# Mask loads moved from the POOL queue to the SP queue in a two-layer masked attention kernel

## The chip, the cores and the metric

The kernel runs on one NeuronCore of one Trainium2 chip. The metric is device time in microseconds (us) of one execution. A profile is one execution recorded instruction by instruction; its span runs from the first to the last instruction. The engines are PE (matrix multiply), PEld (its weight loads, which overlap it), DVE (vector), ACT (scalar, activations), POOL (GpSimd) and SP, which here issues transfers and nothing else. Transfers are issued from the instruction streams of SP, POOL and ACT, in the order in which each stream holds them.

## The reference

Sixteen graphs of 1024 nodes with 256 features, each with a 1024x1024 matrix of 0 and 1, go through two layers of attention. In both the input is normalised and passed through a ReLU, and a score counts only where the matrix is not 0. Layer 0 has 4 heads of 64, layer 1 has 8 heads of 32. All numbers are 32-bit floats; the adjacency is 32-bit integers.

```python
def layer(x, adj, H, Wq, Wk, Wv, Wo, bo):
    h = jnp.maximum(_layernorm(x), 0.0)
    q, k, v = heads(h @ Wq), heads(h @ Wk), heads(h @ Wv)     # layer 1 adds biases
    s = jnp.where(adj > 0, einsum('bhnd,bhmd->bhnm', q, k) / sqrt(256 / H), -inf)
    o = einsum('bhnm,bhmd->bhnd', softmax(s), v)
    return x + concat(o) @ Wo + bo
```

## The kernel before

**Steps.** The attention of one graph is cut into groups: two halves of 512 queries (`qh` 0 and 1) times two groups of heads (`g` 0 and 1). A group runs over its keys in steps of four 128x512 score blocks, 4 steps a group in layer 0 and 8 in layer 1, so a graph has 16 steps of layer 0 and 32 of layer 1. The order of all 768 steps is: layer 0 of graph 0, then, for each graph b, layer 0 of graph b+1 followed by layer 1 of graph b. A period is therefore 48 steps: 16 of layer 0, then 32 of layer 1. In the code `a` is the step at which a period's layer 0 begins, `c = a + 16` the one at which its layer 1 begins; this text counts steps as a+n and c+n. In layer 0 two steps are handled at once and called a pair here.

**A step.** PE computes scores into PSUM (line 454), DVE combines them with the mask (line 477) into a tile p, ACT takes the exponential in place (line 483), and two steps later PE multiplies p with the values (line 495). Scores share three PSUM pairs with every other product, so PE's next scores wait until DVE has read older ones. The row sums of p, which the softmax divides by, come from adding p tiles: on DVE and POOL in layer 0 (lines 504 to 510), on POOL in layer 1 (line 608), where further tiles are added by an accumulating DMA (`accumulate`, line 591) before PE sums over keys (`count`, line 347). `spread`, `invert`, `fetch` and `normalize` (lines 363 to 406) then carry the sums through DRAM: SP transfers sums, vd and inv, and POOL multiplies the head outputs `cat` by inv (line 406). `end_half` (line 431) multiplies by Wo, adds to x and, in layer 1, stores the result (line 444).

**The masks.** A graph's mask comes in eight parts. `Mask.load` (line 143) fetches one part, `put` (line 156) turns it on ACT into an 8-bit form for layer 0, `flip` (line 169) transposes it in blocks on DVE, `second` (line 172) rewrites it on ACT for layer 1. The load is a DMA of the POOL queue that converts 32-bit integers to bf16 as it moves them, into one of two buffers of the pool `adjp`. The first graph's eight parts go to two `p` buffers that are still unused.

**Order.** Each step holds a list of further work, filled by `later(step, function, ...)`; `Stream.run` works it off behind the step's exponentials, large products last. Each engine then runs its instructions strictly in the order in which they were written. The step numbers at lines 766 to 819 are set by hand: when a mask part is loaded, put and flipped, when x is loaded (`open_x`, line 132), when its statistics (`stats`, line 186, DVE) and norms (line 207, ACT) are taken. In before, the parts of the mask of graph b+2 are loaded at a+4, a+8, a+12, c+1, c+12, c+16, c+20 and c+24, each put five steps later and flipped one after that. The second half of x of graph b+2 is loaded at a+14, and the first half of its statistics stands at c (at c+3 in the first period).

**The first accumulating DMA.** In `count_steps` (line 594) a group's first accumulating DMA is issued at its step j=3, with the POOL additions of that step, except in the group with `qh` and `g` both 0: there it is put at the head of the list two steps later.

## Time and profile before

| what | value |
|---|---|
| time, median of 3 runs | 3191.39 us (3191.0 to 3192.33) |
| the profiled execution's own time | 3184.43 us |
| its span | 3182.7 us, 45121 instructions |
| PE busy | 3119.6 us, 98% |
| POOL / DVE / ACT busy | 80% / 79% / 70% |
| mask loads on POOL (line 149) | 128, 207.6 us busy |
| mask puts on ACT (line 164) | 128, 145.2 us busy |
| mean granted PE clock | 0.997 |

A row of the groups gives a line's busy time and the mean duration of one instruction, then the idle time of its engine just before it and what ended it. A row of the timeline gives start and duration in us, engine, line, operation, output and inputs, the number of merged instructions, and in brackets the idle time before it with its releaser. A fp32 product counts as two instructions, and ends of products are modelled, so PE is best read from start to start: the time from one row's start to the next row's start is what the first one took of PE. A window's row gives the window, its length, and the busy time and instructions of PE, PEld, DVE, ACT and POOL in it, then the granted PE clock, the share of the DMA engines and GB/s.

### The profile page before, as it was taken

Reading aid. Unit: us, or ns where it says so; the run is one execution under the profiler, and the core shown is the slowest. Engines: PE = TensorE matmul, PEld = TensorE weight load, DVE = VectorE, ACT = ScalarE, POOL = GpSimd, SP = SyncE. Lnnn points to the kernel's source line nnn. Section 1 sums busy time; section 2 is a strip of 40 time slices with the busy share of each in tenths; the row PEclk is TensorE's granted clock in tenths of the full one; section 3 lists DMA queues with packets and bytes.
Section 4 is the critical chain, followed back from the end, with each engine's and each line's share of the span. In section 5 each row is a group of like instructions: output and inputs, shape, how many; then the busy total and the mean of one; then the engine's idle time right before and its main releaser. Section 6 shows DMA issues by size and latency. Waiting matters only on the chain.

```text
span 3182.7 us, 45121 instructions
## 1 busy us (share of the span) xinstructions
PE 3119.6 (98%) x16662; PEld 1221.8 (38%) x16662; DVE 2521.7 (79%) x2882; ACT 2236.4 (70%) x2440; POOL 2540.5 (80%) x1358
## 2 busy tenths in 40 slices
PE   8989999999999999999999999999999999999998
PEld 3433333434334343333433334333343433434332
DVE  6678788887878878788887878878888787887776
ACT  5657767686676766767677686776768667676765
POOL 5568788797887978878788797878879788796776
PEclk9999999999999999999999999999999999999999
DMA  7216556364563745636355463555636446372421
GB/s 94 34 31 123 105 103 115 76 130 91 104 117 80 132 85 104 126 83 126 85 110 113 89 122 82 113 104 104 115 76 130 91 102 118 83 132 68 87 61 32
DMA packets 449684, 308.46 MB, mean 97 GB/s; under 512 B 248752, under 2 KB 408752, under 8 KB 432432
## 3 DMA queue, kind: packets, MB, share of 16 engines
q0 software_dynamic: 283344, 173.82, 33.8%
q1 hardware_dynamic: 166112, 131.68, 15.1%
q8 instruction: 133, 2.18, 0.3%
q14 instruction: 95, 0.78, 0.1%
HBM read 149.95 MB, written 47.96 MB: 62 GB/s over the span
## 4 chain that ended last, share of the span: by engine, by line
PE 79%; DMA 8%; DVE 7%; issue 2%; SPq 1%; POOL 1%; ACT 1%; DVEq 0%; POOLq 0%; ACTq 0%
PE ps L454 27%; PE po L495 23%; PE pq L270 11%; PE py L436 7%; PE pv L306 6%; PE pz L347 4%; DMA p<-p 4%; DVE p L477 3%; DMA out_dram<-x 3%; DMA x<-in_x_dram 1%; POOL p L608 1%; DVE p L507 1%; DVE st L195 1%; DVE p L504 1%; SPq L444 1%
## 5 line engine op out<-in xcount | busy, mean ns | idle before, releaser
L483 ACT ACTIVATE p<-p 128x1024 f32<-128x1024 f32 x1536 | 1613.0, 1056 | 722.0 <-DVE p L477 662.1
L477 DVE SCALAR_TENSOR_TENSOR p<-mask,ps 128x1024 f32<-128x1024 fp8e5 x1536 | 1786.2, 1214 | 373.8 <-PE ps L454 360.0
L608 POOL TENSOR_TENSOR p<-p,p 128x1024 f32<-128x1024 f32 x510 | 1217.8, 2449 | 135.9 <-PE po L495 115.8
L454 PE MATMUL ps<-qT,kT 32*128 32x512 f32 (+1 forms) x6144 | 1125.3, 628 | 19.7 <-DVE p L477 15.9
L495 PE MATMUL po<-p,v 128*32 128x512 f32 (+1 forms) x6144 | 981.0, 600 | 3.1 <-ACT cat L358 2.8
L454 PEld LDWEIGHTS ps<-qT,kT 32*128 32x128 f32 (+1 forms) x6144 | 380.8, 184 | 694.9 <-issue 288.8
L495 PEld LDWEIGHTS po<-p,v 128*32 128x32 f32 (+1 forms) x6144 | 233.6, 118 | 684.6 <-issue 468.2
L508 POOL TENSOR_TENSOR p<-p 128x1024 f32<-128x1024 f32 x128 | 302.5, 2363 | 89.0 <-DVE p L507 83.6
L507 POOL TENSOR_TENSOR p<-p,p 128x1024 f32<-128x1024 f32 x64 | 150.7, 2355 | 200.1 <-DVE p L504 120.3
L406 POOL TENSOR_TENSOR cat<-cat,inv 128x512 f32<-128x512 f32 x127 | 193.0, 1566 | 91.9 <-DMA inv<-vd 89.8
L270 PE MATMUL pq<-hT,wk 128*128 128x512 f32 x512 | 238.4, 609 | 2.7 <-DMA hT<-turned 1.6
L306 PE MATMUL pv<-wv,hT 128*128 128x256 f32 x1024 | 237.8, 385 | 0.1
L270 PE MATMUL pq<-hT,wq 128*128 128x512 f32 x512 | 236.6, 605 | 0.1
L436 PE MATMUL py<-wo,cat 128*128 128x256 f32 x1008 | 234.0, 385 | 1.2 <-DVE p L477 1.2
L306 PEld LDWEIGHTS pv<-wv,hT 128*128 128x128 f32 x1024 | 189.4, 190 | 72.1 <-DVE p L477 25.0
L436 PEld LDWEIGHTS py<-wo,cat 128*128 128x128 f32 x1008 | 186.6, 190 | 73.3 <-issue 35.1
L149 POOL DMA_DIRECT2D adj<-in_adj_dram x128 | 207.6, 1622 | 4.6 <-issue 4.0
L504 DVE TENSOR_TENSOR p<-p 128x1024 f32<-128x1024 f32 x128 | 171.0, 1336 | 0.0
L347 PE MATMUL pz<-p,ones 128*32 128x512 f32 x1248 | 163.4, 596 | 7.6 <-DMA p<-p 6.8
L592 POOL DMA_DIRECT2D p<-p x133 | 121.8, 916 | 53.1 <-POOL p L608 19.5
L441 DVE TENSOR_TENSOR x<-py,x 128x1024 f32<-128x1024 f32 x63 | 76.9, 1221 | 101.7 <-PE py L436 100.7
L223 POOL TENSOR_TENSOR x<-x,bo 128x1024 f32<-128x1024 f32 x64 | 156.9, 2512 | 0.0
(51 smaller groups left out, 1750.9 us busy)
## 6 DMA issues: line engine op xcount, KB each, us to landing
p<-p POOLq DMA_DIRECT2D x133, 1024.0 KB, 8.1
adj<-in_adj_dram POOLq DMA_DIRECT2D x128, 256.0 KB, 9.7
turned<-hn SPq DMA_DIRECT2D x58, 512.0 KB, 3.5
hT<-turned SPq DMA_DIRECT2D x232, 128.0 KB, 5.3
x<-in_x_dram SPq DMA_DIRECT2D x128, 128.0 KB, 2.8
inv<-vd SPq DMA_DIRECT2D x128, 128.0 KB, 2.9
inv<-vd SPq DMA_DIRECT2D x252, 64.0 KB, 4.8
out_dram<-x SPq DMA_DIRECT2D x124, 128.0 KB, 2.8
```

Source lines behind the costliest of these rows:

```text
L149: nc.gpsimd.dma_start(at, rows[u // 4, u % 4])
L270: nc.tensor.matmul(pq[:, m, :], wt[self.layer][:, c, ts(m, P)], self.hT[half][:, c, :], start=(c == 0), stop=(c == 1),)
L306: nc.tensor.matmul(pv[:, i, :], self.hT[half][:, c, ts(i, P)], w.v[self.layer][:, c, :], start=(c == 0), stop=(c == 1),)
L347: nc.tensor.matmul(self.s[ts(r, 32), :], w.ones.to_broadcast([P, 32]), of, start=start, stop=stop)
L436: nc.tensor.matmul(py[:, i, :], self.half.cat[:, c, ts(i, P)], w.o[self.layer][:, c, :], start=(c == 0), stop=(c == 1),)
L454: nc.tensor.matmul(st.ps[i // 2][:, i % 2, :], gr.inp.kT[r * D : (r + 1) * D, gr.g, ts(kt, P)], gr.inp.qT[gr.qh][r * D : (r + 1) * D, gr.g ...
L477: nc.vector.scalar_tensor_tensor(out=half, in0=gr.mask.m[gr.qh][:, kt // 4, :, kt % 4].unsqueeze(1).to_broadcast([P, 2, 512]), scalar=-EDG ...
L483: nc.scalar.activation(half, half, AF.Exp, scale=gr.scale)
L495: nc.tensor.matmul(gr.o[r * D : (r + 1) * D, :], gr.inp.v[:, kt, h * D : (h + 1) * D], st.halves[i // 2][:, i % 2, :], start=(kt == 0), st ...
L504: nc.vector.tensor_add(a, a, b)
L508: nc.gpsimd.tensor_add(a, a, b)
L608: nc.gpsimd.tensor_add(half, half, of)
```

## The change

The mask load becomes a plain copy of 32-bit integers issued by SP, into a buffer of 4 KB a partition; with the same memory there is one such buffer where there were two of bf16. `put` reads the integers. The first graph's parts go to four `p` buffers; four of the eight are issued by ACT, four by SP. Loads, puts and flips have new steps: the loads of graph b+2 stand at a+6, a+8, a+10, a+12, a+14, c+29 (of the same period), and a+1, a+3 of the next, each put at the step of the next load, in front of it. All but the one at c+29 stand in a layer 0. `second` is spread more widely. The second half of x is loaded at c, behind the layer 0's `inv` in SP's order, and the first half of its statistics moves from c to c+2. The first accumulating DMA of layer 1 is issued at j=3 in every group. The sums of the last graph, which borrow the mask buffer, follow the new buffer count.

```diff
-    adjp = ctx.enter_context(tc.tile_pool(name="adjp", bufs=2))
+    adjp = ctx.enter_context(tc.tile_pool(name="adjp", bufs=1))
...
-        def load(self, u, at=None):
+        def load(self, u, at=None, by=nc.sync):
 
             if at is None:
-                at = adjp.tile([P, 4, 256], BF16, tag="adj", name=f"adj_{self.b}_{u}")
+                at = adjp.tile([P, 4, 256], I32, tag="adj", name=f"adj_{self.b}_{u}")
             self.src[u] = at
             rows = adj[self.b].rearrange("(t h r g) (k c) -> h t k r g c", h=QH, r=32, g=4, k=4)
-            nc.gpsimd.dma_start(at, rows[u // 4, u % 4])
+            by.dma_start(at, rows[u // 4, u % 4])
...
                 elif j == 3:
-                    if gr.qh or gr.g:
-                        self.accumulate(one, gr.one)
-                    else:
-                        self.due.setdefault(i + 2, []).insert(0, (self.accumulate, (one, gr.one)))
+                    self.accumulate(one, gr.one)
...
-    stage = [pp.tile([P, 4, 4, 256], BF16, tag="p0", bufs=7, name=f"adj_0{i}") for i in range(2)]
+    stage = [pp.tile([P, 2, 4, 256], I32, tag="p0", bufs=7, name=f"adj_0{i}") for i in range(4)]
 
     def load(u):
-        masks[0].load(u, stage[u // 4][:, u % 4])
+        masks[0].load(u, stage[u // 2][:, u % 2], nc.scalar if u < 4 else nc.sync)
...
     for t in range(NT):
         i = 5 + 2 * t
-        later(i - 3, masks[1].load, t)
+        later(i - 2, masks[1].load, t)
         later(i, masks[1].put, t)
-        later(i + 1, masks[1].flip, t)
+        later(i + 2, masks[1].flip, t)
...
-        for i, u in zip((0, 1, 2, 3, 4, 6, 8, 10), range(NT)):
+        for i, u in zip((0, 2, 4, 6, 7, 9, 11, 13), range(NT)):
             later(a + i, masks[b].second, u)
         if b + 2 < B:
             other, mask = inputs[0][b + 2], masks[b + 2]
             later(a + 6, open_x, b + 2, 0)
-            later(a + 14, open_x, b + 2, 1)
+            later(c, open_x, b + 2, 1)
...
-                norms(other, 1, c, c + 4, c + 5, c + 6, bias=c + 36)
+                norms(other, 1, c + 2, c + 4, c + 5, c + 6, bias=c + 36)
                 block_inputs(other, 1, c + 7, c + 8, c + 12, c + 22, c + 26, c + 30)
-            for i, t in zip((9, 13, 17, 22, 33, 37, 41, 45), range(NT)):
-                later(a + i - 5, mask.load, t)
-                later(a + i, mask.put, t)
-                later(a + i + 1, mask.flip, t)
+            at = 6, 8, 10, 12, 14, 45, 49, 51, 53
+            for t in range(NT):
+                later(a + at[t], mask.load, t)
+                later(a + at[t + 1], mask.put, t)
+                later(a + at[t + 1] + (1 if t == 4 else 2), mask.flip, t)
```

More of the change, by code (lines that the diff above doesn't have):

```diff
@@ L368, in spread @@
             if k == 0:
-                pool, tag, bufs = small, f"sums{self.layer}", 1
+                pool, tag = small, f"sums{self.layer}"
                 if self.layer and inp.b == B - 1:
-                    pool, tag, bufs = adjp, "adj", 2
+                    pool, tag = adjp, "adj"
                 inp.sums = pool.tile(
-                    [P, (4 if self.layer else 2) * self.n_f], F32, tag=tag, bufs=bufs,
+                    [P, (4 if self.layer else 2) * self.n_f], F32, tag=tag, bufs=1,
                     name=f"sums_{inp.n}",
```

## The prediction

> **What bounds the kernel now.** I read the page first (which engine is full), then the windows of one period (does the bound change by stage), then PE's timeline from start to start (where PE loses time although it counts as busy), then DVE, POOL and SP around those places. The page:

> ```profile
> PE 3119.6 (98%) x16662; PEld 1221.8 (38%) x16662; DVE 2521.7 (79%) x2882; ACT 2236.4 (70%) x2440; POOL 2540.5 (80%) x1358
> ...
> L149 POOL DMA_DIRECT2D adj<-in_adj_dram x128 | 207.6, 1622 | 4.6 <-issue 4.0
> ```

> PE is the bound. The mask loads are 208 us of POOL, but POOL is idle for a fifth of the span, so that time is not itself on the path. The windows of one period (layer 0 is the first two):

> ```profile
> 915.60:954.40 38.80, 38.80 (x172) 15.31 (x168) 27.81 (x27) 26.04 (x28) 31.09 (x16) 1.00 0.50 98
> 954.40:992.00 37.60, 37.60 (x176) 16.18 (x172) 31.15 (x40) 26.04 (x29) 27.12 (x14) 1.00 0.37 76
> 992.00:1014.00 22.00, 21.23 (x106) 8.10 (x104) 15.96 (x18) 12.53 (x15) 14.93 (x7) 1.00 0.33 103
> 1014.00:1045.00 31.00, 30.52 (x177) 11.69 (x174) 26.21 (x29) 21.46 (x24) 27.10 (x17) 1.00 0.55 109
> 1045.00:1111.00 66.00, 66.00 (x422) 24.40 (x421) 56.92 (x70) 53.22 (x59) 60.03 (x34) 1.00 0.66 118
> ```

> Layer 0 has no idle PE at all; what there is lies in the first 50 us of layer 1. PE's rows there:

> ```profile
> 1001.30 2.26 PE L454 MATMUL ps<-qT,kT 32*128 32x512 f32 x8
> 1003.56 3.72 PE L306 MATMUL pv<-wv,hT 128*128 128x256 f32 x16
> 1008.04 2.26 PE L454 MATMUL ps<-qT,kT 32*128 32x512 f32 x8 [0.76 <-DVE p L477]
> 1010.23 1.92 PE L495 MATMUL po<-p,v 128*32 128x512 f32 x16
> ...
> 1020.73 1.85 PE L454 MATMUL ps<-qT,kT 32*128 32x512 f32 x8
> 1022.58 3.70 PE L270 MATMUL pq<-hT,wq 128*128 128x512 f32 x8
> ...
> 1040.27 1.06 PE L495 MATMUL po<-p,v 128*32 128x512 f32 x8
> 1041.79 1.07 PE L347 MATMUL pz<-p,ones 128*32 128x512 f32 x8 [0.46 <-DMA p<-p]
> ```

> Eight score instructions take 1.07 us from start to start where nothing holds them (1012.09 to 1013.16 us); pv takes 3.65 (961.99 to 965.64). So the rows lose 2.26 − 1.07 = 1.19, 4.48 − 3.65 = 0.83 and 2.19 − 1.07 = 1.12 us at c+2 and c+3, 0.78 us at c+6 (1020.73), and 0.46 us in the wait of the row sums at c+11. The same subtraction over eleven periods gives, per period, 2.2 us at c+2 and c+3, 0.8 at c+6, and 1.5 in four small stalls of 0.37 late in layer 1. Nearly all else runs at PE's pace. DVE and SP say why:

> ```profile
> 999.94 0.43 DVE L195 BATCH_NORM_STATS2 st<-x 128x6 f32<-128x256 f32 x1 [3.31 <-DMA x<-in_x_dram]
> 1004.75 2.11 DVE L507 TENSOR_TENSOR p<-p,p 128x1024 f32<-128x1024 f32 x1
> 1016.88 2.18 DVE L199 TENSOR_TENSOR ve<-mv,numbers 128x4 f32<-128x4 f32 x1
> ...
> 994.47 1.75 SPq L135 DMA_DIRECT2D x<-in_x_dram  x4
> 996.27 0.43 SPq L389 DMA_DIRECT2D vd<-vn  x1
> 999.98 2.40 SPq L398 DMA_DIRECT2D inv<-vd  x4
> ...
> 1003.73 4.26 POOL L406 TENSOR_TENSOR cat<-cat,inv 128x512 f32<-128x512 f32 x2 [6.60 <-DMA inv<-vd]
> ```

> DVE stands still for 3.31 us because x's second half has not landed, and the mask step for c+1 (1001.18 us) is queued behind those statistics. The x load stood in SP's queue until an earlier store had landed (the waits give SP at line 135 100.5 us for out_dram), and vd and inv stood behind it; so POOL waits 6.60 us and its two multiplications then meet DVE's additions.

> **The change part by part** (times per period of about 194 us; fourteen periods load masks, thirteen have the statistics at c.)

> *x's second half and its statistics.* The statistics leave c, so DVE's wait there goes. The next candidate for lateness is PE itself: the scores of c+1 end at about 997.7, so line 477 can start there instead of at 1001.18, 3 us earlier. The x load now follows inv: vd no longer waits behind x, so inv is issued about 3 us earlier (from 999.98), x follows at about 999.5 and lands 2.8 us later (its median), near 1002.5; its first reader stands behind c+2's mask steps, which end not before 1004. The gain is between 0 and 13 × 2.2 = 28.6 us. What can take it back is the meeting of DVE's two additions with POOL's two multiplications, which come earlier too: L507 takes 2.11 us here and 1.22 elsewhere, 0.9 us lost, on a DVE that is now 3 us ahead. I take 1.8 of the 2.2: 23 us.

> *First accumulating DMA.* Its issue moves from c+7 (1033.12 us) to behind the POOL additions that begin at 1020.40 and end at 1025.10, 8 us earlier. It landed 8.1 us after issue (median), just too late; now it lands with 8 us to spare. The page's waits give PE 6.8 us in 13 such waits. The 0.9 us that its issue costs POOL only moves, ahead of additions that wait for PE until 1028.49. Between 0 and 6.8; I take 6.5.

> *The stall at c+6.* DVE is late there because L199, 4 columns wide, took 2.18 us while POOL ran an addition from 1014.35 to 1019.03; L201, as wide, took 0.15. POOL loses its 1.60 us mask load at 1012.73 and starts that addition earlier, and DVE arrives earlier: whether they meet again is open. Between 13 × 0.8 = 10 us gained and, if a block as long arises at a second place, 10 lost. I take half of the gain, 5. [...]

> *Mask loads.* 120 parts leave POOL: 120 × 1.62 = 195 us that PE never waited for; DVE waited for POOL's line 608 only 6.7 us in all. I take 1 us. On SP each load costs an issue of about 0.45 us (the four x issues take 1.75). ACT's puts keep their 1.13 us (no row reads integers; the same instruction takes 1.13 from 8-bit and 1.06 for fp32 exponentials; lower bound nothing changed, upper a few tenths, covered below). Per period five puts and five flips move from layer 1 into layer 0: 5 × 1.14 us of ACT and 5 × 0.43 of DVE. There ACT is busy 26 of 38 us and DVE 28 and 31, and pair by pair a gap takes them: at a+10 ACT idles 1.67 us ahead of the exponentials at 975.29, for a 1.13 us `second`. Cost 0; if the cover goes, up to 5.7 us of ACT per period.

> *Waits that are added.* With one buffer, a load waits for ACT's put of the part before it. Behind the load at a+8 in SP's queue stands inv of the last group (issued at 962.69, with its put now ending at about 962.8): it goes out about 1 us later and POOL's line 406 (969.66) and then the py product (981.07) have 11 us. Behind the load at a+14 stands vd of layer 0 (996.27 before); its put ends near 993. The tightest landing is the load of a+6: it goes out behind x at about 957.2, and its put stands at about 961.65, 4.4 us later; ACT then has 1.5 us idle before line 310. A 512 KB transfer of the SP queue (turned) lands in 3.5 us (2.6 to 5.8), 128 KB of x in 2.8, 256 KB of mask on POOL's queue in 9.7. I take 4, the SP rows being nearest: cost 0. From 5.9 us on it costs PE.

> *The start.* Four issues on ACT, about 0.45 each, lie in its idle 7.30 us before the first norm and 1.42 before the first copy; four SP issues delay x of graph 1, needed only at 48 us. PE runs without a gap from 27 to 38 us with either. Layer 0's stalls up to 330 us (some 12 us above a later period) shift by −5 to +3; I take −1.

> Sum: 23 + 6.5 + 5 + 1 + 1 = 36.5, less 1.5 for ACT and SP delays that I can't place: 35 us. The profiled execution took 3184.4 us, 7.0 below the median of the runs; taken off the median, 3191.4 − 35 = 3156. About 0.2% (6.4 us) is what a measurement here can tell from no change.

> **Rivals.**
> 1. The blocks come back: DVE and POOL meet at c+2 and at c+4 as before, and only the accumulating DMA and half of the x wait show. For it: L199's row. Against it: 3 us of DVE lead. 6.5 + 6.5 = 13: 3178.
> 2. All of it goes, with c+6 entirely and the start's 5 and two of the four 0.37 us stalls, since five puts and flips leave layer 1: 28.6 + 6.8 + 10 + 5 + 14 × 0.74 = 61: 3130. Against it: the same 0.37 stalls recur in the last graph, which loads no masks.
> 3. Slower: the 512 KB loads land late. At the 9.7 us of the old queue, the put at a+8 waits 5.3 us, of which ACT's idle covers 1.5 to 2.8; the put at a+10 follows its load by 9 us and loses about 3.5, the next about 1: some 7.5 us × 14 = 105, less 35: 3261. It decides from a landing of about 5.9 + 2.5 = 8.4 us.

> **How the numbers follow.** Forecast (3143 to 3169) 0.50; rival 1 0.18; rival 2 0.17; rival 3 0.08; changes that nearly cancel 0.04, and small losses 0.03. Rival 1's small side and the cancelling case give 0.07 for the same; rival 3 and the losses 0.11 for slower; faster is 0.82. The range from 3126 to 3186 takes in both nearer rivals and leaves out the late landing.

> **What would show it.** Right: no DVE wait for x at c; inv issued before x and POOL's 6.60 us wait shorter by about 3; the scores at c+2 and c+3 at 1.1 to 1.5 us; no wait of line 347 for p; mask loads landing in 3 to 5 us. Wrong: line 164 waiting for adj, PE idle in layer 0, or L504, L507 or L199 at 2 us in new places.

## The result, and the profile after

The changed kernel takes 3460.78 us (median of 4 runs, 3456.3 to 3469.73) against 3191.19 us before (3190.6 to 3192.33): ratio 1.0848, 95% interval 1.0825 to 1.0870. It is 270 us slower where 35 us faster were predicted. Its profiled execution took 3462.27 us, with a span of 3460.5 us and a mean granted PE clock of 0.966 (0.997 before).

The page of the changed kernel, with the rows that answer to those of before:

```profile
PE 3207.1 (93%) x16662; PEld 1244.7 (36%) x16662; DVE 2526.3 (73%) x2882; ACT 2236.4 (65%) x2440; POOL 2310.9 (67%) x1230
...
L164 ACT ACTIVATE mask<-adj,numbers 128x1024 fp8e5<-128x1024 int32 x128 | 146.6, 1148 | 348.9 <-DMA adj<-in_adj_dram 348.9
```

POOL is relieved as announced (2540.5 to 2310.9 us busy), and `put` costs the same from integers (1148 ns against the 1.13 us assumed). But ACT now waits 348.9 us for mask parts, and PE is idle for 7% of the span (2% before), now in layer 0 too, where the windows of before show none. The windows of one period (window and length; then busy PE, PEld, DVE, ACT, POOL; granted clock, DMA share, GB/s; layer 0 is the first three):

```profile
1002.00:1040.80 38.80, 33.70 (x133) 12.79 (x130) 23.65 (x21) 20.71 (x22) 29.56 (x15) 0.91 0.52 118
1040.80:1078.40 37.60, 31.88 (x135) 13.65 (x135) 24.62 (x30) 22.96 (x24) 13.22 (x7) 0.91 0.35 94
1078.40:1094.50 16.10, 16.10 (x76) 6.67 (x72) 13.09 (x18) 12.03 (x14) 9.61 (x6) 1.00 0.25 74
1094.50:1130.00 35.50, 33.24 (x157) 14.07 (x156) 24.76 (x30) 18.34 (x21) 20.62 (x12) 0.90 0.29 85
1130.00:1217.00 87.00, 86.66 (x545) 31.18 (x543) 72.28 (x83) 65.42 (x74) 72.32 (x40) 1.00 0.52 114
```

Three of the five windows have idle PE and a clock of 0.90 or 0.91. The late part of layer 1 (the last row) is as full as it was. The timeline of ACT and of PE in the second window:

```profile
1052.22 4.51 ACT L483 ACTIVATE p<-p 128x1024 f32<-128x1024 f32 x4 [0.56 <-DVE p L477]
1064.75 1.15 ACT L164 ACTIVATE mask<-adj,numbers 128x1024 fp8e5<-128x1024 int32 x1 [8.01 <-DMA adj<-in_adj_dram]
...
1067.32 1.00 ACT L310 COPY v<-pv 128x1024 f32<-128x1024 f32 x1
...
1075.10 1.15 ACT L164 ACTIVATE mask<-adj,numbers 128x1024 fp8e5<-128x1024 int32 x1 [0.74 <-DMA adj<-in_adj_dram]
```

```profile
1057.01 3.72 PE L306 MATMUL pv<-wv,hT 128*128 128x256 f32 x16
1060.66 1.99 PE L454 MATMUL ps<-qT,kT 64*128 64x512 f32 x8
1068.37 3.56 PE L454 MATMUL ps<-qT,kT 64*128 64x512 f32 x8 [5.72 <-ACT v L310]
```

`put` stands at the head of ACT's work for the pair. It waits 8.01 us for its part; the copy of v out of PSUM (line 310) stands behind it, and PE's next scores need that PSUM, so PE stands still for 5.72 us. The timeline of SP, DVE and POOL around c gives the second way:

```profile
1053.26 0.63 SPq L149 DMA_DIRECT2D adj<-in_adj_dram  x1
...
1065.92 0.61 SPq L149 DMA_DIRECT2D adj<-in_adj_dram  x1
...
1096.91 0.62 SPq L149 DMA_DIRECT2D adj<-in_adj_dram  x1
1097.64 1.17 SPq L389 DMA_DIRECT2D vd<-vn  x1
1106.02 2.43 SPq L398 DMA_DIRECT2D inv<-vd  x4
1108.55 1.95 SPq L135 DMA_DIRECT2D x<-in_x_dram  x4
...
1113.47 0.43 DVE L195 BATCH_NORM_STATS2 st<-x 128x6 f32<-128x256 f32 x1 [4.81 <-DMA x<-in_x_dram]
...
1109.62 1.27 POOL L406 TENSOR_TENSOR cat<-cat,inv 128x512 f32<-128x512 f32 x1 [6.67 <-DMA inv<-vd]
```

A load issued at 1053.26 us is put at 1064.75, 11.5 us later; the next one, issued at 1065.92, at 1075.10, 9.2 us later. The transfer vd, 8 KB, goes out 0.7 us behind a load; inv, which needs it, follows 8.4 us after it (3.7 us in before, 996.27 to 999.98), x behind inv, and DVE waits 4.81 us for x at c+2. So DVE's wait of 3.31 us at c, which the change was to remove, has come back two steps later, and longer. The waits over the whole execution:

```profile
ACT mask L164 <- DMA adj<-in_adj_dram: 348.9, 94, 13.4
POOL cat L406 <- DMA inv<-vd: 324.0, 52, 17.1
...
DVE st L195 <- DMA x<-in_x_dram: 76.0, 15, 10.3
...
PE pz L347 <- DMA p<-p: 33.0, 13, 4.2
```

The second and third of these rows in before:

```profile
POOL cat L406 <- DMA inv<-vd: 89.8, 27, 6.6
...
DVE st L195 <- DMA x<-in_x_dram: 37.5, 15, 4.3
```

The last row has moved. In before the 13 waits of line 347 (6.8 us in all) stand at c+11, for a group's first accumulating DMA; now at least 12 of 13 stand at a+5, for the last one of the layer 1 before. POOL and PE in the first window:

```profile
1022.02 1.19 POOL L592 DMA_DIRECT2D p<-p  x1
...
1035.20 1.93 PE L347 MATMUL pz<-p,ones 128*32 128x512 f32 x8 [4.19 <-DMA p<-p]
```

By the landings on record this DMA of POOL's queue lands 11.1 us after its issue, 8.1 in before and 8.5 in the run with four DMAs by keys below (medians of eleven periods), and it is issued 20.6 us after a instead of 16.2. So beside these loads a transfer of another queue is late, too.

**PE's lost time by place.** The same subtraction as in the prediction (start to start, less the unhindered duration), in us per period, means over eleven periods; the runs are those of the next section:

| kernel | a+2 to a+5 | a+8 to a+11 | a+12 to a+15 | c, c+1 | c+2, c+3 | c+4 | c+6 | c+11, c+12 | c+23 to c+31 | all | first scores at |
|---|---|---|---|---|---|---|---|---|---|---|---|
| before | 0.1 | 0 | 0 | 0 | 2.3 | 0 | 0.8 | 1.0 | 1.1 | 7.5 | 37.7 |
| changed | 6.1 | 9.6 | 0 | 1.1 | 0.1 | 4.9 | 0 | 0.9 | 1.2 | 25.9 | 56.3 |
| four DMAs by keys | 0.1 | 1.0 | 0 | 0 | 0.1 | 0.1 | 0 | 0.9 | 1.2 | 5.4 | 46.6 |
| put of a constant | 0.1 | 0 | 8.4 | 0 | 0.1 | 1.9 | 0 | 0.9 | 1.2 | 14.7 | 56.9 |
| loads spread | 0.1 | 0 | 0 | 0 | 0.1 | 0.7 | 0 | 13.1 | 10.3 | 26.4 | 57.8 |
| spread, clear of vd | 0.1 | 0 | 0 | 0 | 0.1 | 1.0 | 0 | 0.9 | 10.9 | 15.0 | 56.0 |
| x alone | 0.1 | 0 | 0 | 0 | 0.3 | 0 | 0 | 1.0 | 1.1 | 4.7 | 37.3 |

Two things are read from the first two rows. What the change was to remove (2.3 at c+2 and c+3, 0.8 at c+6) is gone. And 21.6 us have come in layer 0 and up to c+4, where the loads now stand; 13 periods of 18.4 more make 239 us, and the later start 18.6. Part of it is the clock: the trace's clock records hold 41 stretches at half speed, of 3.4 or 6.8 us but for four (before has 4 stretches). Half of their length is 118.6 us against 11.5, an upper bound for what they cost, since PE idles in some of it.

The late start stands in ACT's rows, the last of them from before:

```profile
2.17 2.60 ACTq L149 DMA_DIRECT2D adj<-in_adj_dram  x1
...
23.92 6.87 ACTq L149 DMA_DIRECT2D adj<-in_adj_dram  x2
30.82 1.01 ACT L237 COPY hT<-ph 128x1024 f32<-128x1024 f32 x1 [14.09 <-issue]
...
13.10 1.01 ACT L237 COPY hT<-ph 128x1024 f32<-128x1024 f32 x1 [1.42 <-PE ph L236]
```

ACT's third load goes out at 23.92 us; by the semaphore records its second, issued at 2.17, has just landed then (23.90). The fourth takes 6.3 us to issue, and the copy for PE's first product stands behind both.

**Why the loads are late.** A load's source is ordered keys (4), rows (32), row groups (4), columns (256), the four key quarters slowest. In the packet records of the load issued at 1065.92 there are 512 packets of 1 KB, 46 ns each by median, from 1067.32 to 1074.56 us. By mean 4.0 of them are under way at once, and between 1067.8 and 1074.0 mostly four or five. The semaphore records fit that. Each of SP's 1422 DMAs in before updates its semaphore 16 times; each of the 128 loads of the changed kernel does so five times, once 1.0 us after its issue (median) and four times at its end, this one at 1066.94 and then at 1074.31, 1074.46, 1075.02 and 1075.07 us. And a transfer behind a load waits for those four: of the 16 updates of the vd issued at 1097.64, behind the load of 1096.91, twelve are in after 2.2 us, and the last four come at 1104.91, 1105.50, 1105.51 and 1105.96, each 0.17 to 0.19 us after one of the load's four (1104.73, 1105.31, 1105.33 and 1105.79). Of 304 transfers issued behind a load at least 3 us before it lands, 284 look like that: twelve updates before the load's four, each of the last four behind one of them. The records name no engine; that the four are four of the 16 DMA engines, and that the four entries of the slowest dimension make them four, is my estimate from these counts.

### The profile page after: what moved, and what is told of

Read it like the earlier page. It is cut to its first block, busy times and chain, and to the rows that moved or that the text cites. A ratio compares the mean times of both kernels' runs of the same rounds, so it can differ in the third digit from the quotient of the medians.

```text
span 3460.5 us, 45072 instructions
## 1 busy us (share of the span) xinstructions
PE 3207.1 (93%) x16662; PEld 1244.7 (36%) x16662; DVE 2526.3 (73%) x2882; ACT 2236.4 (65%) x2440; POOL 2310.9 (67%) x1230
## 3 DMA queue, kind: packets, MB, share of 16 engines
q1 hardware_dynamic: 230096, 196.70, 20.6%
q8 instruction: 133, 2.18, 0.3%
## 4 chain that ended last, share of the span: by engine, by line
PE 50%; DMA 30%; DVE 6%; SPq 4%; POOL 4%; issue 3%; ACT 3%; ACTq 0%; DVEq 0%; POOLq 0%
PE ps L454 16%; PE po L495 13%; DMA adj<-in_adj_dram 12%; PE pq L270 8%; PE py L436 6%; DMA vd<-vn 6%; DMA p<-p 5%; DVE p L477 4%; PE pz L347 3%; PE pv L306 3%; POOL p L608 3%; DMA sums<-s 2%; DMA inv<-vd 2%; SPq L379 1%; SPq L398 1%
## 5 line engine op out<-in xcount | busy, mean ns | idle before, releaser
L477 DVE SCALAR_TENSOR_TENSOR p<-mask,ps 128x1024 f32<-128x1024 fp8e5 x1536 | 1789.8, 1215 | 511.9 <-PE ps L454 469.8
L454 PE MATMUL ps<-qT,kT 32*128 32x512 f32 (+1 forms) x6144 | 1165.3, 641 | 157.2 <-ACT v L310 92.2
L495 PE MATMUL po<-p,v 128*32 128x512 f32 (+1 forms) x6144 | 996.6, 607 | 3.1 <-ACT cat L358 2.9
L454 PEld LDWEIGHTS ps<-qT,kT 32*128 32x128 f32 (+1 forms) x6144 | 382.1, 187 | 856.6 <-issue 349.1
L495 PEld LDWEIGHTS po<-p,v 128*32 128x32 f32 (+1 forms) x6144 | 237.0, 119 | 706.4 <-issue 514.1
L406 POOL TENSOR_TENSOR cat<-cat,inv 128x512 f32<-128x512 f32 x127 | 166.1, 1314 | 326.9 <-DMA inv<-vd 324.0
L164 ACT ACTIVATE mask<-adj,numbers 128x1024 fp8e5<-128x1024 int32 x128 | 146.6, 1148 | 348.9 <-DMA adj<-in_adj_dram 348.9
L507 POOL TENSOR_TENSOR p<-p,p 128x1024 f32<-128x1024 f32 x64 | 151.0, 2359 | 235.2 <-DVE p L504 198.6
L436 PE MATMUL py<-wo,cat 128*128 128x256 f32 x1008 | 254.9, 410 | 10.2 <-DVE p L477 10.2
L270 PE MATMUL pq<-hT,wk 128*128 128x512 f32 x512 | 239.3, 610 | 14.9 <-ACT hT L237 13.8
L306 PE MATMUL pv<-wv,hT 128*128 128x256 f32 x1024 | 237.8, 385 | 0.0
L436 PEld LDWEIGHTS py<-wo,cat 128*128 128x128 f32 x1008 | 201.9, 206 | 99.6 <-DVE p L477 34.7
L270 PE MATMUL pq<-hT,wq 128*128 128x512 f32 x512 | 236.6, 605 | 0.0
L306 PEld LDWEIGHTS pv<-wv,hT 128*128 128x128 f32 x1024 | 189.4, 190 | 71.5 <-issue 13.2
L347 PE MATMUL pz<-p,ones 128*32 128x512 f32 x1248 | 175.5, 633 | 33.8 <-DMA p<-p 33.0
L504 DVE TENSOR_TENSOR p<-p 128x1024 f32<-128x1024 f32 x128 | 194.0, 1516 | 1.2 <-PE po L495 1.2
```

The lines of the kernel that those rows point to most:

```text
L270: nc.tensor.matmul(pq[:, m, :], wt[self.layer][:, c, ts(m, P)], self.hT[half][:, c, :], start=(c == 0), stop=(c == 1),)
L306: nc.tensor.matmul(pv[:, i, :], self.hT[half][:, c, ts(i, P)], w.v[self.layer][:, c, :], start=(c == 0), stop=(c == 1),)
L347: nc.tensor.matmul(self.s[ts(r, 32), :], w.ones.to_broadcast([P, 32]), of, start=start, stop=stop)
L406: nc.gpsimd.tensor_mul(o, o, inv)
L436: nc.tensor.matmul(py[:, i, :], self.half.cat[:, c, ts(i, P)], w.o[self.layer][:, c, :], start=(c == 0), stop=(c == 1),)
L454: nc.tensor.matmul(st.ps[i // 2][:, i % 2, :], gr.inp.kT[r * D : (r + 1) * D, gr.g, ts(kt, P)], gr.inp.qT[gr.qh][r * D : (r + 1) * D, gr.g ...
```

## The experiments

All comparisons are with the kernel before on the same chip. Changed lines are shown against the changed kernel where nothing else is said.

**Is it the number of engines?** Two splits into four DMAs of 128 KB on the same queue at the same steps, one by key quarters, one by row groups, which keeps the four quarters as the slowest dimension.

```diff
-            by.dma_start(at, rows[u // 4, u % 4])
+            for k in range(4):                                    # first run
+                by.dma_start(at[ts(k, 32)], rows[u // 4, u % 4][k])
+            for g in range(4):                                    # second run
+                by.dma_start(at[:, g], rows[u // 4, u % 4][:, :, g])
```

> The changed kernel with each mask load issued as four DMAs, one for each quarter of the keys (32 partitions each, 128 KB), in the same place. Theory A (the load's slowest dimension has 4 entries, so it runs on 4 of the 16 DMA engines, lands after 9 us instead of 4, and holds up what follows in SP's rings): the load spreads as x's four DMAs do (32 partitions each, landing 2.8 us after issue), lands some 4.5 us after its first issue, ACT's 349 us of waiting for adj falls below 60, and the time is about 3156 (3130 to 3185). Theory B (the single buffer makes SP wait for ACT's puts, and that holds up vd and inv whatever the landing): still above 3300. Theory C (the puts and flips are too much for ACT and DVE in layer 0): 3230 to 3300, with no wait for adj.

> The changed kernel with each mask load issued as four DMAs of 128 KB too, but cut along the four interleaved rows, so that each piece still has a slowest dimension of 4. Control for e1: as many issues, as many bytes and packets of the same size. Theory A: every piece stays on 4 engines, the load lands after 9 to 10 us, ACT waits 300 to 450 us for adj, time 3430 to 3520. If the size of one DMA and not its spread is what matters, this is as fast as e1.

By keys: 3170.87 us (3169.74 to 3172.54), ratio 0.9941 (0.9924 to 0.9957). By row groups: 3394.15 us (3386.01 to 3408.43), ratio 1.0654 (1.0625 to 1.0684). The page of the first and the waits of the second:

```profile
L165 ACT ACTIVATE mask<-adj,numbers 128x1024 fp8e5<-128x1024 int32 x128 | 145.4, 1139 | 28.4 <-DMA adj<-in_adj_dram 28.4
...
adj<-in_adj_dram SPq DMA_DIRECT2D x496, 128.0 KB, 3.0
```

```profile
POOL cat L407 <- DMA inv<-vd: 296.3, 55, 14.5
ACT mask L165 <- DMA adj<-in_adj_dram: 289.9, 82, 11.4
```

In the first, a DMA lands 3.0 us after its issue (median), and in an undisturbed load all 512 packets lie between 973.53 and 976.37 us, 9.9 under way by mean. In the second a load's packets take from 998.49 to 1005.76 us with a mean of 3.8, as in the changed kernel. Same bytes, same count of DMAs, same order: 223 us lie between them, so what makes the loads late is how few packets are under way at once (3.8 against 9.9), and not the size of a DMA, their number or the queue. Nor is it the single buffer: the first run has it too, and SP still stands 277.1 us at its loads for ACT's puts. Splitting by row groups helps by 67 us, less than a quarter of what by keys does, but more than the 31 us at most that I had expected; where these come from is not shown. The 3170.87 is above the 3156 that I had expected because the start is still 9 us late (first scores at 46.6 us: the first parts go through 16 issues on ACT and 16 on SP) and 1.0 us a period is left at a+10.

**Does another queue help?** All loads issued by ACT, but for four of the first graph's, which stay on SP.

```diff
-        def load(self, u, at=None, by=nc.sync):
+        def load(self, u, at=None, by=nc.scalar):
```

> The changed kernel with all mask loads issued by ACT instead of SP, in the same places. Theory A: the landing stays at about 9 us, so ACT's waits for adj stay near 350 us and the stall at a+10 (9 us a period) with them; vd, inv and x are no longer behind the load in SP's order, so the x wait and the stall at c+4 (about 5 us a period with the slow clock behind it) shrink: 3350 to 3430. Theory B (SP's order is the cause): about 3160 to 3200.

3419.47 us (3412.47 to 3420.76), ratio 1.0712 (1.0693 to 1.0731). ACT waits 291.3 us for adj, 90 times. It doesn't separate the queue from the landing: SP still waits for loads that it no longer issues (at line 135 122.6 us, at 379 102.1, at 444 49.5). By the semaphores in the instruction records, the DMAs of SP and those of ACT count on the same eight.

**Which way does a late load cost, the put or the queue?** Five runs on the steps and the queue of the loads, then one that takes the put's wait away. In the two on POOL the first graph's loads go to POOL as well.

```diff
-            at = 6, 8, 10, 12, 14, 45, 49, 51, 53
+            at = 5, 9, 13, 17, 22, 33, 37, 41, 45     # spread on SP; the same with by=nc.gpsimd on POOL
+            at = 6, 8, 10, 12, 20, 45, 49, 51, 53     # fifth load behind x
+            at = 5, 9, 13, 17, 28, 33, 37, 41, 45     # spread, clear of vd at c+6
```

> The changed kernel with its loads spread again: puts at the steps at which before had them (a+9, 13, 17, 22, 33, 37, 41, 45) and each load one put earlier, so that 4 steps (some 16 us or more) cover a landing of 9 us. My theory (a load runs on few DMA engines, lands after 9 us, and holds up both ACT's put and what stands behind it in SP's queue): ACT's wait for adj falls from 349 to under 40 us, the stall at a+10 and the half-clock stretch behind it go, but loads in front of vd, inv and x still delay those, so a stall at c+1 to c+4 may stay: 3240 (3170 to 3330). Rival (the number of loads in SP's queue is what costs, not how close each is to its put): the stalls only move, 3400 or more.

> The changed kernel with one load moved: the fifth from a+14, where vd, inv and x stand behind it in SP's queue, to a+20, behind them. By my theory the stalls at c+1 and c+4 (5.7 us a period by the changed kernel's trace, and the half-clock stretch that follows them) go, while the wait at a+10 stays: 3461 less 13 x 5.7 = 74, less up to 13 x 1.5 = 20 for the clock: 3375 (3350 to 3410); POOL's wait for inv falls from 324 us to about 100. Rival (those stalls come from ACT being late since a+10): 3450 or more.

The spread kernel takes 3474.71 us (3459.32 to 3481.44), ratio 1.0875 (1.0852 to 1.0897): my theory missed by 235 us. The half of it that concerns ACT held in the main (adj 95.9 us, 34 waits, where I expected under 40; next to nothing lost from a+2 to c+3). But 12.8 us a period are lost at c+12, and 9.2 more than before from c+23 on. The timeline of SP and POOL shows how those at c+12 come about:

```profile
1135.53 0.61 SPq L149 DMA_DIRECT2D adj<-in_adj_dram  x1
1136.24 5.36 SPq L389 DMA_DIRECT2D vd<-vn  x1
1148.90 2.43 SPq L398 DMA_DIRECT2D inv<-vd  x4
...
1152.42 1.26 POOL L406 TENSOR_TENSOR cat<-cat,inv 128x512 f32<-128x512 f32 x1 [11.89 <-DMA inv<-vd]
```

A load now stood at c+6, directly ahead of a vd. The issue of vd took 5.36 us, inv went out 12.7 us after it, and POOL's additions, which free the p tiles, stood behind its wait of 11.89 us. With the fifth load moved the time is 3448.66 us (3439.53 to 3452.39), ratio 1.0813 (1.0797 to 1.0830), a miss of 74 us. The 4.9 us at c+4 went to nothing, as expected, but 2.7 us came at c+7 to c+10 and 0.8 at a+10 and a+11: the load moved, and so did most of its cost.

> The changed kernel, all steps as changed, 32-bit loads into the same buffers, but every load issued by POOL's queue: nothing of SP's stands behind a load any more, while each put still follows its load by two steps. With the loads on SP and spread, the stall only moved to where vd and inv stood behind a load, so I now hold two costs apart: puts that come too early, and SP's queue. Expected: POOL's wait for inv falls from 324 to about 100 us and the stalls at c+1 and c+4 go; ACT's wait for adj and the stall at a+10 (9.1 us a period) stay; the start is as before (first scores near 38 us). 3461 less 18 less 13 x 5.7 = 3369 (3310 to 3430). Rival (SP's queue is all of it): 3200 or less. Rival (queue order costs nothing, landing is all): 3420 or more.

> As the run before it, with the loads spread so that about four steps lie between load and put. Neither cost is left: 3161 (3150 to 3190), the same as x's second half with the accumulating DMA and no mask change at all (3153.9) and a few us for POOL's waits on the single buffer. If 32-bit loads, integer puts or the single buffer cost something by themselves, it is over 3200. ACT's wait for adj under 30 us, POOL's for inv under 110.

On POOL at the changed steps: 3477.24 us (3470.96 to 3493.43), ratio 1.0895 (1.0879 to 1.0912). On POOL and spread: 3456.17 us (3452.88 to 3466.27), ratio 1.0832 (1.0816 to 1.0849). Both missed, the second by 295 us. SP's queue was free of loads, and POOL's wait for inv fell to 82.1 us in the first, yet 8.8 us a period were lost at a+2 to a+5 and 5.4 at a+8: POOL itself waits 321.5 us for ACT's puts, since the load waits for the single buffer and POOL's additions stand behind it. In the spread one the landing is longer (11.3 us median) and isn't covered late in layer 1: some 7 us a period are lost at c+11 and c+12 and some 14 from c+23 on. POOL's and ACT's timeline:

```profile
1167.61 0.90 POOL L592 DMA_DIRECT2D p<-p  x1 [0.30 <-POOL p L608]
1168.31 1.63 POOL L149 DMA_DIRECT2D adj<-in_adj_dram  x1
...
1184.84 1.15 ACT L164 ACTIVATE mask<-adj,numbers 128x1024 fp8e5<-128x1024 int32 x1 [6.99 <-DMA adj<-in_adj_dram]
```

By the packet records this load's packets begin at 1175.73 us, 7.4 us after its issue, behind an accumulating DMA of 1 MB on the same queue. Before had the same loads on the same queue with landings up to 20.0 us, but two buffers and five steps of lead.

> The changed kernel with loads on SP and puts at a+9, 13, 17, 28, 33, 37, 41, 45: as in the spread run, but the fourth put and the fifth load stand at c+12 and not at c+6, where the load went out 0.7 us ahead of vd and inv and the scores of c+12 then waited 10.8 us a period (with 2.0 us behind them). If the order in SP's queue made that stall, it goes, and so does POOL's wait for inv of some 10 us a period: 3475 less 13 x 12.8 = 3309 (3270 to 3370); the stalls of 9 us a period from c+23 on stay. Rival (any 512 KB load on four DMA engines costs its 10 us wherever it stands): 3440 or more.

3330.76 us (3318.71 to 3335.98), ratio 1.0454 (1.0437 to 1.0472): within the range. One load moved away from vd at c+6 takes the 13.1 us at c+11 and c+12 down to 0.9 and 144 us off the time; the 10.9 us from c+23 on stay, as I expected.

```diff
-                to, self.src.pop(u).rearrange("p g (h c) -> p g h c", h=2), AF.Identity,
+                to, (... if self.b < 2 else w.edges[:, None, None, :].to_broadcast([P, 4, 2, 128])),
+                AF.Identity,
```

> The changed kernel, every load issued as there and landing in the same buffer, but the puts of graphs 2 to 15 read one constant column instead of the loaded part, so that ACT never waits for a load of theirs; these graphs have all their edges set, which leaves out the use of their mask. It keeps what the loads do to SP's queue and to other transfers, and takes away the late put. If the late put is the greater part: the stalls at a+2 to a+5 (6.1 us a period) and a+10 and a+11 (9.6) go and the clock with them, those at c to c+4 (6.0) stay: 3461 less 13 x 15.7 = 3257 (3230 to 3330), ACT's wait for adj near 10 us. If the loads cost by what they do to other transfers: 3380 or more.

3321.24 us (3310.96 to 3330.7), ratio 1.0424 (1.0392 to 1.0457): 140 us less than the changed kernel, with all its loads; it leaves out the use of the masks of graphs 2 to 15. ACT's wait for adj is 11.6 us, and next to nothing is lost from a+2 to a+11, where the changed kernel loses 15.7 us a period. What is left besides the late start (56.9 us) is 1.9 us a period at c+4, where 4.9 were, and 8.4 at a+13 and a+14, which are new: a load no longer waits for the put before it, so loads go out at other moments too. The 140 us are what remains of both. Timeline of SP and POOL:

```profile
1013.19 1.88 SPq L394 DMA_DIRECT2D vd<-vn  x1
1019.03 0.60 SPq L152 DMA_DIRECT2D adj<-in_adj_dram  x1
1020.71 2.42 SPq L403 DMA_DIRECT2D inv<-vd  x4
...
1029.41 1.27 POOL L411 TENSOR_TENSOR cat<-cat,inv 128x512 f32<-128x512 f32 x1 [11.18 <-DMA inv<-vd]
```

Here inv stands behind a load in the queue and lands 8.7 us after its issue. So both ways are real: with the put's wait a net 140 us go, and where time is still lost, POOL waits for a transfer that stands behind a load.

**Do the other two edits do what was predicted?** Against the kernel before, masks untouched:

```diff
-            later(a + 14, open_x, b + 2, 1)
+            later(c, open_x, b + 2, 1)
...
-                norms(other, 1, c, c + 4, c + 5, c + 6, bias=c + 36)
+                norms(other, 1, c + 2, c + 4, c + 5, c + 6, bias=c + 36)
...
-                    if gr.qh or gr.g:
-                        self.accumulate(one, gr.one)
-                    else:
-                        self.due.setdefault(i + 2, []).insert(0, (self.accumulate, (one, gr.one)))
+                    self.accumulate(one, gr.one)
```

All three hunks, then the first two alone, then the third alone:

> The kernel before with two parts of the change alone: x's second half loaded at c with its statistics at c+2, and layer 1's first accumulating DMA at j=3. The mask loads stay on POOL as they were. By the prediction's terms 23 + 6.5 + 5 us go: 3157 (3143 to 3170). By its first rival (the blocks between DVE and POOL come back) 3178; if both stalls vanish fully 3146.

> The kernel before with x's second half alone: its load at c, behind inv, and its first statistics at c+2; masks and accumulating DMA as before. Prediction's terms: the x part took 23 us, and 5 for the stall at c+6, if that stall comes from DVE being late and not from the moved masks. Together 28 of the 35 us: 3189 less 28 is 3161 (3155 to 3170). If the stall at c+6 went because POOL had no mask load in front of it, it comes back here and the time is 23 below: 3166 or above. Since x and accumulating DMA together gave 35.3 us without any mask moved, I expect the first.

> The kernel before with the first accumulating DMA at j=3 in every group, and nothing else. The prediction's term is 6.5 us (0 to 6.8): 3182.7, ratio 0.998 (0.9975 to 1.0). The rival is that the row sums simply wait at another place, since POOL issues another DMA later: then 3189, ratio 1.0. If the two edits add up, this gain and that of x alone make 35.3 us.

Both edits: 3153.86 us (3153.19 to 3154.95), ratio 0.9887 (0.9871 to 0.9904), 35.3 us. x alone: 3149.30 us (3148.84 to 3149.71), ratio 0.9871 (0.9856 to 0.9886), 40.1 us. The accumulating DMA alone: 3190.59 us (3187.35 to 3195.49), ratio 1.0003 (0.9994 to 1.0012), nothing. The 35.3 us, beside the 34.5 of the prediction's three terms, looked like a confirmation; it was two errors that cancel, 40.1 where the terms say 28 (and I expected at least 3155) and nothing where they say 6.5. That both edits give less than x alone is hardly shown: their intervals overlap. The timelines of POOL and SP, with x alone and with both:

```profile
1016.66 2.71 SPq L398 DMA_DIRECT2D inv<-vd  x4
...
1023.09 0.98 POOL L592 DMA_DIRECT2D p<-p  x1
1023.80 2.83 POOL L406 TENSOR_TENSOR cat<-cat,inv 128x512 f32<-128x512 f32 x2
```

```profile
1019.29 0.99 POOL L592 DMA_DIRECT2D p<-p  x1 [0.30 <-POOL p L608]
...
1020.12 4.32 SPq L398 DMA_DIRECT2D inv<-vd  x4
...
1029.22 2.53 POOL L406 TENSOR_TENSOR cat<-cat,inv 128x512 f32<-128x512 f32 x2 [2.62 <-DMA inv<-vd]
```

Issued early, the accumulating DMA (1 MB) goes out 0.8 us ahead of inv, whose four issues then take 4.32 us instead of 2.71. POOL's product waits for inv until 9.1 us after the first of these issues; with x alone it could begin after 7.1. The row sums no longer wait at c+11 (0.7 us), but the scores of c+12 do (0.7 us).

**A version that beats both.** On top of x alone, the first accumulating DMA stands between the two additions of j=5; and with that, the changed kernel with every repair (four DMAs by keys, first graph's loads on POOL, first load at a+5).

```diff
                     nc.gpsimd.tensor_add(half, half, of)
+                    if j == 5 and k == 0 and not (gr.pairs or gr.qh or gr.g):
+                        self.accumulate(*gr.early)
...
-                        self.due.setdefault(i + 2, []).insert(0, (self.accumulate, (one, gr.one)))
+                        gr.early = one, gr.one
```

> x's second half as in the run with x alone (3149.3), and the first accumulating DMA issued between the two additions of step j=5: after inv has been fetched, but some 2.3 us earlier than in before. In the run with x and the accumulating DMA at j=3, inv's four DMAs took 4.3 us to issue right behind that DMA instead of 2.7, POOL waited 2.6 us for inv, and the 0.7 us that the row sums no longer waited came back as 0.7 us at the scores of c+12. If that is so, both go here: 14 x 0.7 = 10 us, 3140 (3136 to 3146). Rival (whatever is issued there delays POOL by as much): 3149.

> The changed kernel with each load in four DMAs by key quarter on SP (3170.9 when that alone was changed), the first graph's eight loads as single 32-bit DMAs of POOL's queue (start as before: 9 us), the first load of a period one step earlier (the last 1.0 us at a+10 gone: 14 us), and the accumulating DMA between the additions of j=5 (10 us): 3138 (3130 to 3152). Against the run with x and the same accumulating DMA, it shows what moving the mask loads off POOL is worth once they land in time: my prediction's term was 1 us; between 10 us gained and 10 lost.

The first: 3140.72 us (3139.51 to 3141.01), ratio 0.9846 (0.9833 to 0.9860), the best kernel of this study. Its timeline of POOL:

```profile
1019.05 0.98 POOL L592 DMA_DIRECT2D p<-p  x1
1019.76 2.67 POOL L608 TENSOR_TENSOR p<-p,p 128x1024 f32<-128x1024 f32 x1
1022.10 2.81 POOL L406 TENSOR_TENSOR cat<-cat,inv 128x512 f32<-128x512 f32 x2
```

The product no longer waits, and the waits at c+11 and c+12 are both gone. The second: 3147.43 us (3146.88 to 3148.42), ratio 0.9867 (0.9852 to 0.9882), 6.7 us slower than the first. Their periods are alike (most between 190.7 and 191.5 us); 4.4 us of the difference are there when the second layer 0 begins (120.93 against 116.57 us). So in these two kernels moving the mask loads off POOL is worth nothing, even when they land in time.

## Why the prediction was wrong, point by point

- **The step that failed** is the landing in "waits that are added": "I take 4, the SP rows being nearest: cost 0." The loads land after 9 us or more. Two rows were at hand: a turned transfer of the same size on SP's queue at 3.5 us, and the same rows of adj on POOL's queue at 9.7. I took the queue for what sets the landing; it is the access pattern, which the second row shares and the first doesn't: on SP's queue a load cut by keys had 9.9 packets under way, cut by row groups 3.8. The packet records of before could have told: a turned transfer takes 2.0 us with 10 packets under way, a load of adj 6.9 us with 4.8 (medians). Rival 3 carried the right number (9.7) and the bound from which it decides (8.4), and I gave it 0.08.
- **Rival 3 was too small as well.** It priced the put's wait at 105 us; taking that wait away is worth a net 140. It had no term for what stands behind a load, nor for the accumulating DMA of POOL's queue beside it. The step "Behind the load at a+14 stands vd of layer 0 (996.27 before); its put ends near 993" counted only until when SP waits to issue, not how late the transfers behind it land: POOL's wait for inv went from 89.8 to 324.0 us. Nor had it a term for the clock, which fell to half in 41 places.
- **The start.** Taken as a gain of 1 us, it was a loss of 18.6. "Four issues on ACT, about 0.45 each" took 1.15, 2.60, 0.55 and 6.27 us, and the third had to wait for the second to land, so that ACT's first copy for PE came 14.1 us late. With all loads on POOL the first scores come at 38.6 to 39.1 us, nearly as before.
- **x's second half** (23) and **the stall at c+6** (5) were undervalued, and one edit makes both: 40.1 us measured. The halving for a block that comes back elsewhere was not needed: with x alone c+2 and c+3 lose 0.3 us a period instead of 2.3, and c+6 nothing. 13 × (2.0 + 0.8) = 36 of the 40 us. The blocks did come back in good part: DVE's lines 504, 507 and 199 take 171.0, 89.9 and 40.5 us in before and 176.6, 88.1 and 26.4 with x alone, 10 us less of 301. But DVE's wait for x went from 37.5 to 7.2 us, and PE waited for hardly any of the blocks. So the first rival's sum of 13 us was wrong, since it took every block to lie on the path; what makes a block (L199 at 2.18 us beside an addition of POOL, 0.16 by median) no run shows. (Its second 6.5 is also not the "half of the x wait" that it is called; half would be 11 to 14.)
- **First accumulating DMA** (6.5): 0. "now it lands with 8 us to spare" fits, since with this edit line 347 no longer waits for p, but what its issue does to inv, the next transfer, was not asked. The step moved past POOL's additions was counted, the queue of SP was not.
- **Mask loads leaving POOL** (1): −7 to 0 by the two last kernels. **Integer puts**: 1148 ns against 1.13 us, right. The puts and flips in layer 0 cost nothing where the loads land in time, as taken: with four DMAs by keys layer 0 loses 1.1 us a period, 1.0 of it at a+10.

What stays open: how the 172 us that are left between the kernel with a constant put (3321) and that with x alone (3149) divide between the order in SP's queue and the four late updates of the transfers beside a load. By the table 13 × 10.3 = 134 lie at a+13, a+14 and c+4, and 20 in the start.

## What to carry to other kernels

The landing time of a load (9 us or more) was to be read here from the row of the same access pattern (9.7 us, on POOL's queue), not from that of the same size and queue (3.5): look at how many packets are under way at once, and if it is few (4.0 here), try a split along the slow dimension, which in the first run made them 9.9 and the landing 3.0 us. That a single DMA with another slowest dimension does as well was not run here. Before a load is moved into a queue, list what is issued behind it within its landing time; a small transfer that others wait for (here vd, inv, x) can pay for it: POOL's wait for inv went from 89.8 to 324.0 us. And a sum that comes out right is no proof of its terms: only the runs of one edit at a time showed 40 and 0 where I had 28 and 6.5.
